# Reordering the border between a spiking recurrence and its score products: halves of the last copy of v, a short early count, and ScalarE's first output copies in a row

## The chip, the cores and the metric

The kernel runs on one core of a Trainium2 chip. The metric is the device time of one execution in microseconds, the median of several runs. One more execution is taken with a profiler, and everything that is read from a trace below comes from it.

## The reference

Sequences of 50 item numbers (1024 of them) are looked up in a table of 100001 rows of 128 values; row 0 counts as zero. The running means over time are normalised over the batch at each step, and drive a membrane that spikes. The mean spike count is multiplied with the whole table.

```python
emb = emb_table.at[0].set(0.0)
e = emb[seq]                                   # 1024 x 50 x 128
prefix = jnp.cumsum(e, axis=1)
denom = jnp.minimum(t_idx[None, :], lengths[:, None])
uF = prefix / denom[:, :, None]
y = (uF - uF.mean(axis=0)) * lax.rsqrt(uF.var(axis=0) + BN_EPS) * gamma + beta
def step(v, x):
    v = v + (x - v) / TAU                      # TAU = 2
    spike = (v - V_TH >= 0)                    # V_TH = 1
    v = v - spike * V_TH
    return v, spike
_, spikes = lax.scan(step, v0, y by time)
uF_out = spikes.mean(axis=0)                   # 1024 x 128
scores = uF_out @ emb.T                        # 1024 x 100001, float32
```

The scores are 409.6 MB, which is nearly all that the kernel writes.

## The kernel before

The work has two stages. In the first, a loop over t = 0 to 49 does the recurrence with the 128 features on the partitions and the 1024 sequences (B) in the columns. For each t, POOL gathers eight tiles of 128 rows (line 196), TensorE transposes and adds them into two PSUM banks pre0 and pre1 (line 310, 512 columns each), VectorE divides by the lengths into uF (line 319) and takes statistics (lines 320 and 326), ScalarE takes the square root r (line 330). VectorE then works out the scale a in a few instructions on one column, ScalarE writes x into a PSUM tile v (line 360), VectorE adds the old membrane (`step`, line 363). Three things are made of v: ScalarE's copy d = v − 1 as bf16 (`over`, line 282), VectorE's negv, which holds the reset membrane with its sign turned (`rest`, line 286), and VectorE's running count of spikes (`spiked`, line 289). In the loop, count and negv of step t are done during step t+1, behind other work. The v tiles alternate between the two PSUM tags v0 and v1, of two banks each; step 48 lies in v0.

The last step (t = 49) has its own order. The spikes of the first 128 sequences are worked out first (vA, countA), so that the first products can start; the next 512 (countB, through the bank of pre1) and the last 384 (countC, through a PSUM tile vC) follow. Before the products, TensorE does 16 transposes into a tile called warm, which nothing reads.

In the second stage, the table is taken in parts of 1024 rows: TensorE transposes them, ScalarE writes a high part (line 146) and VectorE a low part (line 147), and for each of eight groups n of 128 sequences, four matmuls of 512 columns (line 154, `product`) make a block of 128 × 1024 scores in PSUM. A block is copied out, times 1/50, by VectorE (line 486) or ScalarE (line 488) in turn, by the parity of the counter `turn`. The copies go into a tile o, and SP issues the store of it (line 163). Parts are taken in groups of WIDTHS = four of 2, four of 3 and thirteen of 6, and the loop over n is inside that over the groups, so a store carries 2, 3 or 6 blocks. Group n = 0 of the first two parts is done ahead, in halves of 512 columns, by `first_store` (lines 409 to 414): three of its copies on ScalarE, the fourth on VectorE. Its PSUM tiles are po_0_0 (tag po0) and po_0_1.

The order is written by hand (`manual_schedule`): each engine executes its instructions in the order of the program, and semaphores are added for what depends on another engine. The PSUM pool of the second stage has four buffers of two banks; they reuse the banks of the first stage, and each waits for the last user of what lay there.

## Time and profile before

| | |
|---|---|
| time, median of 3 runs | 1636.69 us (1634.44 to 1641.79) |
| profiled execution | 1575.79 us, of which the span is 1573.8 us |
| busy: PE, DVE, ACT, POOL | 1128.7, 944.8, 668.2, 380.4 us |
| output copies, line 486 (VectorE) and 488 (ScalarE) | 391 each, 1.22 and 1.02 us on average for one |
| HBM written, read | 409.60 MB, 77.69 MB |
| stores of 3 MB | 96, 20.0 us from issue to landing (median) |
| first store issued | 513.48 us after the span's start |

Engines: PE is TensorE's matmul, PEld its weight load, DVE is VectorE, ACT is ScalarE, POOL is GpSimd, SP issues the stores. A busy share over the whole span mixes the two stages; the stages have to be read apart. In the row of slices, each digit is the busy share in tenths of a fortieth of the span (39.3 us).

### The profile page before, as it was taken

To read this page: it belongs to the slowest core of one execution; us is meant where nothing else is said; L and a number is where in the kernel's file an instruction comes from. 1 tells how busy PE (TensorE), PEld (TensorE's weight loads), DVE (VectorE), ACT (ScalarE), POOL (GpSimd) and SP (SyncE) were. 2 spreads that over 40 slices of the span, in tenths; PEclk is the share of its full clock that TensorE was granted. 3 is DMA by queue.
4 is the path that set the end of the run, shared out by engine and by line. 5 is a ranking of instruction groups with operands and counts; after the bars stand their busy time and mean duration, and the time that the engine had idled before them with its cause. 6 is when DMAs were issued, how large, how long until landed. Compare 5 with 4: busy or idle time off the path is not lost.

```text
span 1573.8 us, 12233 instructions
## 1 busy us (share of the span) xinstructions
PE 1128.7 (72%) x4450; PEld 801.0 (51%) x4450; DVE 944.8 (60%) x1126; ACT 668.2 (42%) x697; POOL 380.4 (24%) x406
## 2 busy tenths in 40 slices
PE   4544444444444998889878878787888788888884
PEld 2211111111122776668666666666666666666663
DVE  5777777777777665567545545555555545555552
ACT  2333333333333554456444444444444444444542
POOL 7777777777776000000000000000000000000000
PEclk7555555555555999999999999999999999999998
DMA  9611111111121999999999999999999999999898
GB/s 349 235 52 54 52 54 52 53 53 53 52 80 45 373 415 404 422 416 403 422 427 432 431 427 425 421 413 432 412 429 425 413 428 410 426 413 425 379 426 371
DMA packets 51897, 488.12 MB, mean 310 GB/s; under 512 B 10075, under 2 KB 11004, under 8 KB 30588
## 3 DMA queue, kind: packets, MB, share of 16 engines
q1 hardware_dynamic: 30464, 429.81, 64.9%
q0 software_dynamic: 12800, 26.24, 5.7%
q10 hardware_dynamic: 8572, 31.28, 5.0%
q8 instruction: 35, 0.57, 0.1%
q14 instruction: 26, 0.21, 0.0%
HBM read 77.69 MB, written 409.60 MB: 310 GB/s over the span
## 4 chain that ended last, share of the span: by engine, by line
DMA 51%; POOL 18%; PE 11%; issue 8%; ACT 5%; DVE 3%; another core or an unknown queue 1%; ACTq 0%; SPq 0%; POOLq 0%; DVEq 0%
DMA scores<-o 46%; POOL e L196 18%; PE po L154 11%; DMA e<-in_L_rec_emb_table,idx 5%; ACT o L488 5%; DVE o L486 1%; PE pt L124 0%; ACT pairs L146 0%; DMA idx<-in_r_seq 0%; PE pre L310 0%; ACTq L116 0%; DVE negv L286 0%; DVE bs L320 0%; ACT hi L146 0%
## 5 line engine op out<-in xcount | busy, mean ns | idle before, releaser
L486 DVE TENSOR_SCALAR o<-po 128x1024 f32<-128x1024 f32 x391 | 464.2, 1221 | 346.5 <-DMA scores<-o 304.7
L488 ACT ACTIVATE o<-po 128x1024 f32<-128x1024 f32 (+1 forms) x391 | 389.4, 1018 | 542.5 <-DMA scores<-o 313.6
L196 POOL DMA_INDIRECT e<-in_L_rec_emb_table,idx x400 | 379.8, 949 | 123.8 <-issue 112.8
L154 PE MATMUL po<-pairs,countB 128*128 128x512 f32 x1136 | 305.4, 415 | 64.4 <-ACT o L488 49.2
L310 PE MATMUL pre<-ident,e 128*128 128x128 f32 x400 | 179.8, 462 | 228.9 <-DMA e<-in_L_rec_emb_table,idx 228.3
L154 PEld LDWEIGHTS po<-pairs,countB 128*128 128x128 f32 x1136 | 219.3, 198 | 127.8 <-ACT o L488 63.9
L154 PE MATMUL po<-pairs,countC 128*128 128x512 f32 x852 | 233.8, 421 | 46.6 <-ACT o L488 46.5
L310 PEld LDWEIGHTS pre<-ident,e 128*128 128x128 f32 x400 | 73.3, 184 | 338.8 <-DMA e<-in_L_rec_emb_table,idx 338.1
L154 PEld LDWEIGHTS po<-pairs,countC 128*128 128x128 f32 x852 | 165.2, 200 | 91.7 <-ACT o L488 57.6
L147 DVE TENSOR_TENSOR pairs<-pt,pairs 128x1024 fp32r<-128x1024 f32 x71 | 86.3, 1222 | 93.0 <-ACT pairs L146 93.0
L319 DVE SCALAR_TENSOR_TENSOR uF<-rlen,pre 128x512 f32<-128x512 f32 x100 | 68.3, 683 | 109.0 <-PE pre L310 108.9
L124 PE MATMUL pt<-ident,rows 128*128 128x128 f32 x782 | 110.5, 288 | 8.8 <-issue 4.9
L124 PEld LDWEIGHTS pt<-ident,rows 128*128 128x128 f32 x782 | 100.3, 151 | 27.1 <-issue 12.5
L330 ACT ACTIVATE r<-mv,eps 128x1 f32<-128x1 f32 x50 | 14.8, 295 | 225.0 <-DVE mv L326 225.0
L154 PE MATMUL po<-hi,countB 128*128 128x512 f32 x216 | 91.1, 422 | 18.1 <-ACT o L488 14.6
L270 PE MATMUL pre<-zT,ls 128*128 128x512 f32 x100 | 77.4, 776 | 23.5 <-DVE uF L319 19.6
L154 PE MATMUL po<-lo,countB 128*128 128x512 f32 x216 | 88.4, 411 | 0.0
L282 ACT ACTIVATE d<-v,less 128x1024 bf16<-128x1024 f32 x49 | 54.6, 1113 | 63.5 <-DVE v L363 63.5
L154 PE MATMUL po<-hi,countC 128*128 128x512 f32 (+1 forms) x162 | 68.1, 420 | 14.2 <-ACT o L488 14.1
L146 ACT CAST pairs<-pt 128x1024 fp32r<-128x1024 f32 x71 | 71.8, 1012 | 14.2 <-PE pt L124 14.2
L154 PE MATMUL po<-pairs,countA 128*128 128x512 f32 x284 | 71.3, 394 | 8.2 <-ACT o L488 8.2
L360 ACT ACTIVATE v<-uF,hgb,a 128x1024 f32<-128x1024 f32 x49 | 59.2, 1208 | 30.6 <-DVE a L356 30.5
(76 smaller groups left out, 819.3 us busy)
## 6 DMA issues: line engine op xcount, KB each, us to landing
scores<-o SPq DMA_DIRECT2D x96, 3072.0 KB, 20.0
scores<-o SPq DMA_DIRECT2D x32, 1536.0 KB, 8.9
scores<-o SPq DMA_DIRECT2D x30, 1024.0 KB, 8.0
rows<-in_L_rec_emb_table ACTq DMA_DIRECT2D x19, 1536.0 KB, 29.4
scores<-o SPq DMA_DIRECT2D x8, 2896.5 KB, 17.4
rows<-in_L_rec_emb_table SPq DMA_DIRECT2D x6, 3072.0 KB, 29.3
e<-in_L_rec_emb_table,idx POOLq DMA_INDIRECT x400, 2.5
rows<-in_L_rec_emb_table SPq DMA_DIRECT2D x1, 1024.0 KB, 5.1
```

The costliest lines, as they stand in the source:

```text
L124: nc.tensor.transpose(pt[:, k0 : k0 + kw], r[:kw, k0 : k0 + D], ident[:kw, :kw])
L146: nc.scalar.copy(vh, vp)
L147: nc.vector.tensor_tensor(vl, vp, vh.bitcast(F32), ALU.subtract)
L154: nc.tensor.matmul(po[:, :kw], lhsT=counts[n], rhs=part[:, k0 : k0 + kw], start=j == 0, stop=j == 1,)
L196: nc.gpsimd.indirect_dma_start(out=es[t][:, n * P : (n + 1) * P], out_offset=None, in_=table, in_offset=bass.IndirectOffsetOnAxis(ap=idx[: ...
L270: nc.tensor.matmul(pre[h], lhsT=l, rhs=zT[:, h * BANK : (h + 1) * BANK], start=t == 0, stop=False, skip_group_check=True,)
L282: nc.scalar.activation(d, v, AF.Identity, bias=less)
L310: nc.tensor.matmul(pre[h][:, k : k + P], lhsT=e[:, h * BANK + k : h * BANK + k + P], rhs=ident, start=False, stop=last, is_transpose=True, ...
L319: nc.vector.scalar_tensor_tensor(uF[:, cs], rlen[:, cs], 1.0 / (t + 1), pre[h], ALU.max, ALU.mult)
L360: nc.scalar.activation(vt, uF[:, cs], AF.Identity, bias=hgb[:, 1:2], scale=a)
L486: nc.vector.tensor_scalar_mul(o[:, h0 : h0 + hw], po[:, :hw], 1.0 / T)
L488: nc.scalar.mul(o[:, h0 : h0 + hw], po[:, :hw], 1.0 / T)
```

## The change

ScalarE's copy d of step 48 is made in two halves of 512 columns. In the last step, VectorE counts only the first 128 columns of step 48 at first, and makes negv in two halves, with near (which needs 128 columns of negv) between them. The counts of the other columns of step 48 come later: 512 columns after x of group B has been issued, 384 after the output copies of n = 0. Step 48's v stays in use until then, so the tile warm moves from the tag v0 to po0 (whose banks nothing else has used yet), po_0_1 from v0 to v1, and vC from v1 to v0. ScalarE issues x of group B, then its three output copies in a row, then x of vC; before, each x was followed by one copy. The counter `turn` starts at 1, so that of every pair of blocks ScalarE copies the first and VectorE the second.

```diff
@@ -276,20 +276,22 @@
                     skip_group_check=True,
                 )
 
+        whole = slice(0, B)
+        halves = [slice(h * BANK, (h + 1) * BANK) for h in range(B // BANK)]
+
         def over(t, v):
 
             d = lp.tile([P, B], BF16, tag="d", name=f"d_{t}")
-            nc.scalar.activation(d, v, AF.Identity, bias=less)
+            for cs in halves if t == T - 2 else (whole,):
+                nc.scalar.activation(d[:, cs], v[:, cs], AF.Identity, bias=less)
             return d
 
-        def rest(d, v):
-            nc.vector.scalar_tensor_tensor(negv, d, 0.0, v, ALU.is_ge, ALU.subtract)
+        def rest(d, v, cs):
+            nc.vector.scalar_tensor_tensor(negv[:, cs], d[:, cs], 0.0, v[:, cs], ALU.is_ge, ALU.subtract)
 
         def spiked(out, cs, v):
             nc.vector.scalar_tensor_tensor(out, v, V_TH, count[:, cs], ALU.is_ge, ALU.add)
 
-        whole = slice(0, B)
-        halves = [slice(h * BANK, (h + 1) * BANK) for h in range(B // BANK)]
         v = None
 
         correct(0, only(0))
@@ -299,10 +301,11 @@
             last = t == T - 1
             e = es.pop(t)
             if last:
-                spiked(count, whole, v)
-                rest(d, v)
+                spiked(count[:, :P], slice(0, P), v[:, :P])
+                rest(d, v, halves[0])
                 near = once.tile([P, P], F32, tag="r0", name="near")
                 nc.vector.tensor_scalar(near, negv[:, :P], -0.5, hgb[:, 1:2], ALU.mult, ALU.add)
+                rest(d, v, halves[1])
             uF = up.tile([P, B], F32, tag="uF", name=f"uF_{t}")
             bs = sp.tile([P, B // BANK, 6], F32, tag="bs", name=f"bs_{t}")
             for h, cs in enumerate(halves):
@@ -338,7 +341,7 @@
 
 
             if t and not last:
-                rest(d, v)
+                rest(d, v, whole)
 
             nc.vector.reciprocal(r, r)
             q = sp.tile([P, 1], F32, tag="q", name=f"q_{t}")
@@ -390,16 +393,15 @@
 
 
 
-        warm = vp.tile([P, HALF], F32, tag="v0", name="warm")
+        warm = accp.tile([P, HALF], F32, tag="po0", name="warm")
         for k in range(2 * KQ):
             nc.tensor.transpose(warm[:, k % KQ * P : (k % KQ + 1) * P], ident, ident)
-        vC = vp.tile([P, B - BANK - P], F32, tag="v1", name="vC")
-        groups = [(slice(P, P + BANK), pre[1], countB), (slice(P + BANK, B), vC, countC)]
-        for cs, vt, _ in groups:
+        po1 = vp.tile([P, HALF], F32, tag="v1", name="po_0_1")
+        pieceB, pieceC = slice(P, P + BANK), slice(P + BANK, B)
+        for cs in (pieceB, pieceC):
             nc.scalar.activation(uF[:, cs], uF[:, cs], AF.Identity, bias=mv[:, 0:1], scale=-1.0)
 
         po0 = accp.tile([P, HALF], F32, tag="po0", name="po_0_0")
-        po1 = vp.tile([P, HALF], F32, tag="v0", name="po_0_1")
         o0 = gp.tile([P, HALF], F32, tag="e", name="o_0_0")
         o1 = up.tile([P, HALF], F32, tag="uF", name="o_0_1")
         firsts = [(q, po, o, h, cs) for q, po, o in ((0, po0, o0), (1, po1, o1)) for h, cs in enumerate(halves)]
@@ -413,14 +415,17 @@
                 nc.scalar.mul(o[:, cs], po[:, cs], 1.0 / T)
             store(0, q * HALF + h * BANK, o[:, cs])
 
-        for k, (cs, vt, _) in enumerate(groups):
-            x(vt, cs)
-            first_store(*firsts[k])
-        for cs, vt, c in groups:
-            step(vt, cs)
-            spiked(c, cs, vt)
-        for f in firsts[2:]:
+        x(pre[1], pieceB)
+        spiked(count[:, pieceB], pieceB, v[:, pieceB])
+        step(pre[1], pieceB)
+        spiked(countB, pieceB, pre[1])
+        for f in firsts:
             first_store(*f)
+        spiked(count[:, pieceC], pieceC, v[:, pieceC])
+        vC = vp.tile([P, B - BANK - P], F32, tag="v0", name="vC")
+        x(vC, pieceC)
+        step(vC, pieceC)
+        spiked(countC, pieceC, vC)
 
 
 
@@ -429,7 +434,7 @@
         tc.tile_pool(name="psum", bufs=4, space=bass.MemoryType.PSUM, reuse_waits="tile")
     )
     opening = ExitStack()
-    turn = 0
+    turn = 1
     blocks = 0
     q0 = 0
     to_split = WIDTHS[0]
```

## The prediction

> **What bounds the kernel now.** I read the page first, then the busy time by stage, then the timeline of the few microseconds that the diff touches, then the chain of waits. From the page:

> ```profile
> span 1573.8 us, 12233 instructions
> POOL 7777777777776000000000000000000000000000
> DMA  9611111111121999999999999999999999999898
> ```

> A slice is 39.3 us. There are two stages: until slice 13 the gathers on POOL run and the DMA engines are nearly idle; then POOL stops and the DMA engines are full to the end, writing the 409.60 MB of scores. The change sits on the border. The busy time by stage shows how sharp the border is (the last two columns are DMA share and GB/s):

> ```profile
> 500.00:513.50 13.50, 8.13 (x30) 5.79 (x30) 10.80 (x22) 5.16 (x8) 3.77 (x4) 0.60 0.09 24
> 513.50:520.00 6.50, 5.57 (x24) 4.13 (x23) 4.69 (x7) 3.58 (x5) 0.00 (x0) 1.00 0.76 301
> 520.00:530.00 10.00, 10.00 (x54) 8.42 (x53) 7.06 (x7) 6.14 (x7) 0.00 (x0) 1.00 0.98 401
> 800.00:900.00 100.00, 83.40 (x359) 66.00 (x360) 54.45 (x46) 45.53 (x46) 0.00 (x0) 0.91 1.01 429
> ```

> From 520 us on the transfers set the end. So an edit at the border is worth exactly what it moves the time from which the DMA engines are continuously fed, and nothing more. In 513.5 to 522 us they lie idle for about 2.0 us (summed from narrower windows), so the feed starts, in effect, near 515.5 us. The timeline shows what leads up to it:

> ```profile
> 503.06 1.11 ACT L282 ACTIVATE d<-v,less 128x1024 bf16<-128x1024 f32 x1 [1.29 <-DVE v L363]
> 504.21 1.22 DVE L289 SCALAR_TENSOR_TENSOR count<-v,count 128x1024 bf16<-128x1024 f32 x1 [1.18 <-ACT d L282]
> 505.35 1.21 DVE L286 SCALAR_TENSOR_TENSOR negv<-d,v 128x1024 f32<-128x1024 bf16 x1
> 506.37 0.48 PE L310 MATMUL pre<-ident,e 128*128 128x128 f32 x1 [0.77 <-DMA e<-in_L_rec_emb_table,idx]
> 506.59 0.29 DVE L305 TENSOR_SCALAR near<-negv,hgb 128x128 f32<-128x128 f32 x1
> 506.61 3.28 PEld L395 LDWEIGHTS warm<-ident 128*128 128x128 f32 x16
> 506.80 0.68 DVE L319 SCALAR_TENSOR_TENSOR uF<-rlen,pre 128x512 f32<-128x512 f32 x1
> 508.12 0.67 DVE L319 SCALAR_TENSOR_TENSOR uF<-rlen,pre 128x512 f32<-128x512 f32 x1
> 509.56 0.21 DVE L326 BATCH_NORM_AGGREGATE mv<-bs 128x2 f32<-128x12 f32 x1
> 511.22 0.29 DVE L289 SCALAR_TENSOR_TENSOR countA<-vA,count 128x128 fp32r<-128x128 f32 x1
> 512.86 0.60 ACT L413 ACTIVATE o<-po 128x512 f32<-128x512 f32 x1 [0.38 <-PE po L154]
> 513.35 0.67 ACT L360 ACTIVATE vC<-uF,hgb,a 128x384 f32<-128x384 f32 x1
> 515.12 0.68 DVE L411 TENSOR_SCALAR o<-po 128x512 f32<-128x512 f32 x1
> 515.86 0.50 PE L154 MATMUL po<-hi,countB 128*128 128x512 f32 x1 [0.68 <-DVE o L411]
> ```

> Columns are start, duration, engine and line; the bracket is the idle time before and its releaser. DVE is the bound from 504.21 to 511.5: the eighth transpose of step 49 ends at 506.85, so DVE could read the first half of pre earlier (its transposes ended near 501.9) but is busy with count and negv. Note the 1.18 us in which count waits for ScalarE's d, although it does not use d: both read v.

> [...] the granted clock is 0.60 in 500 to 513.5 us and 1.00 after, so the warm transposes (506.64 to 510.29) must stay where they are, and they do.

> **The change, part by part.**

> 1. *Halved d, short count, halved negv.* Half a d: ScalarE's 1024-column eviction takes 1.03 and its 512-column one 0.60, so 512 columns are 0.43; d's first half ends at 503.06 + 1.11 − 0.43 = 503.74, the second near 504.25 (ScalarE instructions of 512 follow each other in 0.49). So the extra instruction costs 0.1 us at most. On DVE, a 128-column operation holds the engine 0.2 us (near to uF: 506.59 to 506.80), a 512-column one about 0.61 (bs to uF: 507.51 to 508.12). Old queue: count, negv, near from 504.21 to 506.80. New queue: count of 128 (0.23), negv half 0 (0.68, its end is awaited), near (0.21), negv half 1 (0.61), so uF comes 1.76 after the start. The unknown is the start. If count's 128 columns wait for d's first half alone: 503.77, uF at 505.52, second uF at 506.84, but its transpose ends at 506.85, so 506.89: a gain of 508.12 − 506.89 = **1.23**. If they wait for all of d: 504.28, uF 506.04, second uF 507.35: a gain of **0.77**. A hint for the latter: the first output copy (512.86) reads what two products wrote, yet starts when the fourth ends (512.82). A wait there covers a whole tile. I take 0.77 and keep 1.23 as the other bound.
> 2. *warm in po0's banks* removes its wait for negv; it still follows the last transpose. It caps the gain: countA's first matmul (511.66 before) cannot start before warm's end, 510.29, so at most 1.37. Not binding.
> 3. *Rest of count later.* 512 columns (0.61) go into DVE's 0.93 us wait for x of group B: free. The other 384 (0.56) come after VectorE's own output copy, and only vC waits for them.
> 4. *ScalarE's copies in a row.* x(vC) (0.67) leaves its place between the first and second copy. The copies would begin at 512.09, 512.58 and 513.07 (each 0.49; the third needs the eighth product, 513.74 − 0.77 = 512.97), against 512.86, 513.95 and 514.42. VectorE's fourth copy no longer stands behind vC and countC: 513.70 against 515.12. Stores on SP's queue keep their number and order and come 0.77 to 1.4 earlier.
> 5. *The price: vC is late.* It lies in v's old banks, so it waits for the 384-column count: count 514.3, x 514.9 to 515.5, step 515.55, countC 516.15 to 516.70 against 515.21 before. Behind x(vC) on ScalarE stands the copy of block n=1, q=0; behind countC on DVE stands q=1's. PE needs countC first at 523.13, so the count itself has 6 us to spare.
> 6. *turn = 1* swaps the 391 + 391 output copies: q=0 goes to ScalarE (515.55 to 516.57; VectorE ended it at 516.94 before), q=1 to VectorE after countC (516.70 to 517.95, against 518.17). Then n=2: ScalarE 516.7 to 517.7, VectorE 517.9 to 519.1. Its 1 MB store goes at about 519.15 instead of 519.95, and from there the DMA engines are fed. Each group's last copy becomes 1.22 instead of 1.03; a 3 MB store takes about 20 us to land (7.3 at 429 GB/s alone), so two others are queued and hide 0.2. The very last store has no cover: about +0.1.

> Sum: −0.8 + 0.1, about **−0.8** (−1.3 with the other bound). The profiled execution took 1575.79 with a span of 1573.8, and would take 1575.0. The median of the runs shown is 60.9 above it; that lies outside the profile, and I carry the difference over: 1636.69 − 0.8 = **1635.9**.

> **Rivals.**

> *A PSUM buffer takes the place of the wait that went.* Four output buffers lie over the eight banks. Before, the second product of n=1 took the buffer whose last reader was VectorE's fourth copy (last line above, 0.68 us). Were it the same banks again, they now hold vC, and PE waits for countC at 516.2 to 516.7; q=1's copy ends at 518.8, n=2's store goes at 520.65 to 521.1 instead of 519.95: +0.7 to +1.2, **1637.6**, slower. It decides once countC ends later than about 515.5. For it: the same banks were second in line. Against: which buffer is taken is not in the trace.

> *The swap breaks the steady state.* If the 0.2 us of the last copy were not hidden, the 160 stores from the second group on would cost 0.2 each: +32, **1669**. It decides when less than 4.5 us of transfers (the time from a freed buffer to its store, on the chain) is queued. Against: shares of 0.95 to 1.01 in every stretch of 50 us or more from 520 to 1550, and two queued stores. The other way, the stalls that an altered order could close are small: 2.0 us in 710 to 720, 1.1 in 596 to 606 (0.57 share in 1460 to 1470 has stores queued and is the transfers' own).

> *The transfers swallow it*: earlier first stores only widen the gap before n=1, **1636.7**.

> **How the numbers follow.** Forecast 0.5, buffer 0.3, swallowed 0.12, swap slower 0.05, an unknown gain from the swap 0.03. The three runs shown spread over 7.4 us, 0.45%, so 0.5% (8 us) is about what a measurement can tell from no change; all but the last two cases lie inside it. Scatter alone may carry a median out: faster 0.05, same 0.89, slower 0.06. The range takes −1.3 to +1.2 and about 4 to 5 us for the scatter: 1630.5 to 1641.5.

> **What would show it.** Right: d in two rows of 0.7; count's 128 columns at 503.8 or 504.3; second uF at 506.9 to 507.4; first store issued at 512.2 to 512.8 (513.48 before); DMA share near 1 from about 519; later stages alike. Wrong: PE idle over 1 us before n=1's second product with countC as releaser (the buffer rival), or shares under 0.95 after 530 (the swap).

## The result and the profile after

The changed kernel is slower. Over 19 runs each, the median is 1642.73 us against 1638.18; the ratio is 1.0032, with a 95% interval of 1.0020 to 1.0045, so 5.2 us (3.3 to 7.4); the two medians alone differ by 4.55 us. The forecast was 1635.9 with a range to 1641.5. A second comparison gave 1578.63 against 1576.15, ratio 1.0018 (1.0011 to 1.0026), 2.8 us (1.7 to 4.1).

Absolute times can be read only inside one comparison: in some of them the first stage of every kernel, the one before included, is some 60 to 70 us longer, with pauses of POOL between gathers (POOL is idle for 181.8 us before its gathers in the first profile after, for 123.8 in that of before). The profile of before shown above is of the short kind and the first profile after of the long kind; none of before is of the long kind. I therefore count from the end of step 48's v (503.03 us in that profile of before, 564.26 in the one after) and call this "after v".

The timeline of the changed kernel around the border, in order of time, columns as before:

```profile
564.30 1.26 ACT L286 ACTIVATE d<-v,less 128x512 bf16<-128x512 f32 x2 [1.30 <-DVE v L366]
565.05 3.30 PE L398 MATMUL warm<-ident 128*128 128x128 f32 x16
565.60 0.29 DVE L293 SCALAR_TENSOR_TENSOR count<-v,count 128x128 bf16<-128x128 f32 x1 [1.33 <-ACT d L286]
568.64 0.67 DVE L322 SCALAR_TENSOR_TENSOR uF<-rlen,pre 128x512 f32<-128x512 f32 x1
572.17 0.77 PE L154 MATMUL po<-hi,countA 128*128 128x512 f32 x1 [3.82 <-DVE a L355]
572.73 0.63 PE L154 MATMUL po<-lo,countA 128*128 128x512 f32 x1
576.59 0.69 DVE L413 TENSOR_SCALAR o<-po 128x512 f32<-128x512 f32 x1 [2.14 <-ACT o L415]
577.84 0.67 ACT L363 ACTIVATE vC<-uF,hgb,a 128x384 f32<-128x384 f32 x1 [1.28 <-DVE count L293]
579.14 0.56 DVE L293 SCALAR_TENSOR_TENSOR countC<-vC,count 128x384 fp32r<-128x384 f32 x1
579.75 0.50 PE L154 MATMUL po<-hi,countB 128*128 128x512 f32 x1 [2.12 <-DVE countC L293]
579.81 1.03 ACT L493 ACTIVATE o<-po 128x1024 f32<-128x1024 f32 x1 [1.30 <-DVE countC L293]
```

What is to be seen: the short count starts 0.04 us after both halves of d are done, and the second uF starts at 4.38 after v against 5.09 before. So the first part of the change brings 0.71 us. Then two things eat it. TensorE idles 3.82 us before its first product and works at half clock when it comes (0.50 in the table below; 0.63 us for a matmul where before had 0.39). And countC ends at 15.44 after v instead of 12.18; TensorE waits 2.12 us for it before n=1's second product (the four matmuls of its block q=1), and ScalarE waits 1.30 us for it before its first copy of n=1. The stage table of the same kernel says it in two columns (granted clock and DMA share, the third and second from the end):

```profile
572.00:574.00 2.00, 1.83 (x4) 1.49 (x5) 1.63 (x5) 0.78 (x1) 0.00 (x0) 0.50 0.00 0
574.00:576.00 2.00, 2.00 (x6) 1.60 (x5) 0.45 (x1) 1.13 (x3) 0.00 (x0) 0.50 0.13 50
578.00:580.00 2.00, 0.25 (x1) 0.25 (x2) 1.12 (x2) 0.70 (x2) 0.00 (x0) 0.97 0.40 154
580.00:582.00 2.00, 2.00 (x10) 1.60 (x10) 1.02 (x1) 0.93 (x2) 0.00 (x0) 1.00 0.16 63
```

The mark that counts is the store of n=2, the seventh that SP issues: from there on the transfers set the time. In the changed kernel it is this line, 19.85 after v; before it was at 16.93.

```profile
584.11 0.33 SPq L163 DMA_DIRECT2D scores<-o  x1
```

From the seventh store to the end of the span, before took 1573.8 − 519.96 = 1053.8 us and the changed kernel 1637.8 − 584.11 = 1053.7. In all 16 profiles of this study that stretch is 1053.5 to 1054.5. So nothing of the loss lies in the second stage, and 2.9 us of it lie in this profile between v and the seventh store.

### The profile page after: what moved, and what is told of

It reads as the page before. It is cut to its first block, busy times and chain, and to the rows that moved or that the text cites. A ratio compares the mean times of both kernels' runs of the same rounds, so it can differ in the third digit from the quotient of the medians.

```text
span 1637.8 us, 12235 instructions
## 1 busy us (share of the span) xinstructions
PE 1089.5 (67%) x4450; PEld 815.5 (50%) x4450; DVE 947.8 (58%) x1129; ACT 673.1 (41%) x698; POOL 380.8 (23%) x406
## 3 DMA queue, kind: packets, MB, share of 16 engines
HBM read 77.69 MB, written 409.60 MB: 298 GB/s over the span
## 4 chain that ended last, share of the span: by engine, by line
DMA 43%; DVE 18%; PE 15%; another core or an unknown queue 9%; ACT 5%; issue 5%; POOL 4%; ACTq 0%; SPq 0%; DVEq 0%; POOLq 0%
DMA scores<-o 39%; PE po L154 14%; POOL e L196 4%; DVE uF L322 3%; DVE bs L323 3%; DVE o L491 3%; DVE v L366 3%; ACT o L493 2%; DVE negv L290 2%; DMA rows<-in_L_rec_emb_table 2%; DVE count L293 1%; DMA e<-in_L_rec_emb_table,idx 1%; ACT v L363 1%; DVE pairs L147 1%
## 5 line engine op out<-in xcount | busy, mean ns | idle before, releaser
L491 DVE TENSOR_SCALAR o<-po 128x1024 f32<-128x1024 f32 (+1 forms) x391 | 467.5, 1214 | 326.5 <-DMA scores<-o 178.6
L493 ACT ACTIVATE o<-po 128x1024 f32<-128x1024 f32 x391 | 391.7, 1025 | 498.4 <-DMA scores<-o 354.6
L196 POOL DMA_INDIRECT e<-in_L_rec_emb_table,idx x400 | 380.1, 950 | 181.8 <-issue 107.0
L154 PE MATMUL po<-pairs,countB 128*128 128x512 f32 x1136 | 302.3, 412 | 56.1 <-ACT o L493 56.1
L154 PE MATMUL po<-pairs,countC 128*128 128x512 f32 x852 | 241.3, 428 | 60.4 <-ACT o L493 52.8
L154 PEld LDWEIGHTS po<-pairs,countB 128*128 128x128 f32 x1136 | 217.7, 196 | 117.1 <-ACT o L493 72.7
L154 PEld LDWEIGHTS po<-pairs,countC 128*128 128x128 f32 x852 | 167.6, 204 | 111.3 <-ACT o L493 64.5
L270 PEld LDWEIGHTS pre<-zT,ls 128*128 128x128 f32 x100 | 29.2, 293 | 322.3 <-DVE uF L322 290.6
L313 PE MATMUL pre<-ident,e 128*128 128x128 f32 x400 | 122.6, 434 | 69.8 <-DMA e<-in_L_rec_emb_table,idx 47.9
L313 PEld LDWEIGHTS pre<-ident,e 128*128 128x128 f32 x400 | 80.7, 210 | 113.1 <-DMA e<-in_L_rec_emb_table,idx 73.2
L154 PE MATMUL po<-hi,countB 128*128 128x512 f32 x216 | 90.3, 418 | 17.7 <-ACT o L493 15.5
L154 PE MATMUL po<-lo,countB 128*128 128x512 f32 x216 | 87.3, 406 | 0.0
L286 ACT ACTIVATE d<-v,less 128x1024 bf16<-128x1024 f32 (+1 forms) x50 | 54.7, 1096 | 63.5 <-DVE v L366 38.9
L154 PE MATMUL po<-hi,countC 128*128 128x512 f32 (+1 forms) x162 | 68.8, 425 | 14.6 <-ACT o L493 12.6
L363 ACT ACTIVATE v<-uF,hgb,a 128x1024 f32<-128x1024 f32 x49 | 59.2, 1208 | 30.9 <-DVE a L359 14.8
```

What stands on the lines that cost most here:

```text
L154: nc.tensor.matmul(po[:, :kw], lhsT=counts[n], rhs=part[:, k0 : k0 + kw], start=j == 0, stop=j == 1,)
L196: nc.gpsimd.indirect_dma_start(out=es[t][:, n * P : (n + 1) * P], out_offset=None, in_=table, in_offset=bass.IndirectOffsetOnAxis(ap=idx[: ...
L270: nc.tensor.matmul(pre[h], lhsT=l, rhs=zT[:, h * BANK : (h + 1) * BANK], start=t == 0, stop=False, skip_group_check=True,)
L286: nc.scalar.activation(d[:, cs], v[:, cs], AF.Identity, bias=less)
L313: nc.tensor.matmul(pre[h][:, k : k + P], lhsT=e[:, h * BANK + k : h * BANK + k + P], rhs=ident, start=False, stop=last, is_transpose=True, ...
L363: nc.scalar.activation(vt, uF[:, cs], AF.Identity, bias=hgb[:, 1:2], scale=a)
```

## The experiments

My theory: the loss is the late seventh store, from half clock at the first products and from the wait for countC. The rivals: countC alone, and the swap of the output copies (turn = 1). The table collects what was measured; "store" is the seventh store after v in the one profile of each kernel, with its difference to before's 16.93 (a second profile of before has 16.91); "time" is the measured ratio to before in the same comparison, over 13 to 22 runs of the kernel and 19 to 75 of before, and the same in us with its 95% interval.

| kernel | clock at the first products | countC ends | store | time against before |
|---|---|---|---|---|
| changed | 0.50 | 15.44 | 19.85, +2.9 | 1.0032, +5.2 (3.3 to 7.4) |
| changed, second comparison (a_again) | 1.00 | 13.83 | 18.22, +1.3 | 1.0018, +2.8 (1.7 to 4.1) |
| b_warm | 0.50 | 13.05 | 17.89, +1.0 | 0.9999, −0.2 (−2.1 to 1.8) |
| a_near | 1.00, then 0.50 | 14.36 | 18.74, +1.8 | 1.0017, +2.8 (1.0 to 4.8) |
| a_turn0 | 0.50 | 15.43 | 20.92, +4.0 | 1.0027, +4.4 (2.6 to 6.2) |
| a_near_sbuf | 1.00 | 12.93 | 16.25, −0.7 | 1.0006, +1.0 (−0.8 to 2.8) |
| a_near_sbuf_2 | 1.00 | 12.93 | 16.27, −0.7 | 1.0000, 0 (−1.3 to 1.4) |
| b_again | 1.00 | 12.17 | 16.91, 0 | 0.9999, −0.2 (−1.4 to 1.3) |
| b_turn1 | 0.50 | 13.05 | 18.13, +1.2 | 1.0001, +0.2 (−1.3 to 1.4) |
| a_sbuf | 0.50 | 14.54 | 17.87, +0.9 | 1.0003, +0.5 (−0.8 to 1.7) |
| best | 1.00 | 11.71 | 15.79, −1.1 | 0.9993, −1.1 (−2.4 to 0.2) |
| a_near22 | 1.00 | 14.20 | 20.19, +3.3 | 1.0018, +2.8 (1.7 to 3.9) |
| best22 | 1.00 (steps up in the first) | 12.41 | 16.51, −0.4 | 0.9994, −0.9 (−2.4 to 0.3) |
| a_order | 0.50 | 12.34 | 16.79, −0.1 | 1.0000, 0 (−2.5 to 2.5) |
| b_halves | 1.00, then 0.50 | 11.48 | 16.55, −0.4 | 0.9997, −0.5 (−2.3 to 1.3) |

**b_warm**: before, with warm early.

```diff
-        warm = vp.tile([P, HALF], F32, tag="v0", name="warm")
+        warm = accp.tile([P, HALF], F32, tag="po0", name="warm")
```

> The kernel before with one line changed: the tile warm takes the tag po0 instead of v0, so its 16 transposes no longer wait for negv. Clock theory (the change is slower because warm runs too early, the array idles over 3 us before countA's first product, and the products then run at half clock): warm ends about 4 us and more before the first product, the products of n=0 stand 0.43 us apart instead of 0.23, the third output copy comes some 1.6 us later, 1 to 2.5 us slower than before. Buffer theory (only countC's wait costs) and swap theory (only turn=1 costs): the same as before within 0.5 us.

In its profile, warm ends at 0.3 after v, 8.3 us before the first product, and all of n=0 runs at half clock (0.50); the store comes 1.0 us late. The time does not show the 1 to 2.5 us that the clock theory expected (−2.1 to 1.8). Half clock behind an early warm is there; what it costs alone is under 2 us and not shown in the time.

**a_near**: the changed kernel, with warm held until near is written.

```diff
-            nc.tensor.transpose(warm[:, k % KQ * P : (k % KQ + 1) * P], ident, ident)
+            nc.tensor.transpose(warm[:, k % KQ * P : (k % KQ + 1) * P], near, ident)
```

> The changed kernel, but the 16 warm transposes take near as their input instead of the identity, so that they start only when VectorE has written near. What they write is read by nobody. Clock theory: warm starts about 2 us later than in the changed kernel, the clock stays at 1.0 through the first products (0.23 us apart), the third output copy comes 1.6 us earlier, and the kernel is 1.5 to 2 us faster than the changed one, so about 3 us slower than before if the whole loss is 5. Buffer and swap theories: as slow as the changed kernel, ratio 1.003.

Warm starts at 2.60 instead of 0.79 after v and the first four of the eight matmuls of n=0 run at full clock (1.00), the last ones at half (0.50); the store moves from 19.85 to 18.74. The ratio falls from 1.0032 to 1.0017, but the intervals overlap, so the time does not establish the expected gain of 1.5 to 2 us. Slower than before it remains: half clock at the first products is not the whole cause.

**a_turn0**: the changed kernel with `turn = 0`.

> The changed kernel with turn = 0, so that the output copies fall to the engines as they did before. Swap theory (the loss beyond the 2.9 us seen at the border comes from the order of 782 copies): 2 us or more faster than the changed kernel. Clock and buffer theories: the same as the changed kernel within 1 us, ratio 1.003; the second stage, from the store of n=2 to the end, lasted 1053.8 us before and 1053.7 after, which speaks against the swap.

Still 4.4 us slower. The swap theory falls here; b_turn1 below settles it. Its store is the latest of all; in this profile the clock costs twice: n=0 runs at half clock (0.50), the wait for countC is 2.93 us here, and the matmuls behind it are at half clock again (0.63 us).

**a_near_sbuf**, and **a_near_sbuf_2** in another comparison: a_near's edit and

```diff
-        vC = vp.tile([P, B - BANK - P], F32, tag="v0", name="vC")
+        vC = once.tile([P, B - BANK - P], F32, tag="vC", name="vC")
```

> The changed kernel with two edits: warm takes near as its input (as in the other run), and vC is a tile in SBUF instead of PSUM banks 6 and 7, so that the buffer of n=1's second product waits for the 384-column count only and not for countC. Clock and buffer theories together: both losses at the border go (1.6 and about 1.2 to 2 us), and the earlier first output copies are left: n=2's store about 16.2 us after step 48's v, against 16.95 before and 19.8 in the changed kernel; 0.5 to 1 us faster than before. Swap theory: still about 2 us slower than before.

> The changed kernel with warm fed by near and vC in SBUF, a second time, since the first comparison (1.0006, -0.0005 to 1.0017) could not tell 0.7 us faster from 1 us slower. Border theory: 0.3 to 0.8 us faster than before and 2 to 3 us faster than the changed kernel. If ScalarE's copies in a row cost more than the border shows: slower than before.

The wait of the second product shrinks to 0.50 us (it starts at 11.93 after v, when the 384-column count has ended), x of vC no longer waits for that count, and the store goes 0.7 us earlier than before. ScalarE's first copy of n=1 still waits for countC, 1.77 us, so that wait is not one for vC's PSUM banks. In the quieter of the two comparisons the kernel is level with before (−1.3 to 1.4). Against the changed kernel in the same comparison the 2.8 us are gone. Since a_near alone still loses 2.8 us, it is the move of vC into SBUF that takes the loss away. The 0.7 us of gain are neither shown nor excluded.

**b_again**: before, unchanged.

> The kernel before once more, as a measure of what two equal kernels differ by, and for a profile whose first stage is as long as in the other runs (the first profile of before had a first stage some 57 us shorter). All theories: ratio 1.000 within 0.001. Clock theory: warm starts right after negv, 3.6 us after step 48's v, and ends about 1.5 us before the first product, so the products of n=0 stand 0.23 us apart at least at first; n=2's store goes about 17 us after v.

Two equal kernels differ by 0.2 us. Its first stage is short like that of the first profile, so I did not get the long kind that I wanted; its border is the same to 0.02 us.

**b_turn1**: before with `turn = 1`.

> The kernel before with turn = 1 and nothing else: the swap of the output copies alone. The four kernels with the changed border measured 1 to 2.3 us more than the shift of n=2's store in their profiles explains. Swap theory: 1.5 to 2.5 us slower than before, the second stage (from n=2's store to the end) longer by as much. Border theory (clock and countC alone): the same as before within 1 us; n=2's store at about the same time after v.

The swap costs nothing (−1.3 to 1.4). The profile brought something else: up to the first products this kernel has the same instructions as b_again, warm begins 3.7 us after v in both and ends over 1 us ahead of the products in both (1.26 and 1.76), and yet b_again ran them at full (1.00) and b_turn1 at half clock (0.50). The stage tables, first b_turn1 and then b_again, clock in the third column from the end:

```profile
511.00:513.00 2.00, 1.36 (x3) 1.16 (x4) 1.04 (x4) 0.98 (x2) 0.00 (x0) 0.50 0.00 0
513.00:515.00 2.00, 2.00 (x6) 1.55 (x5) 0.96 (x3) 1.28 (x3) 0.00 (x0) 0.50 0.00 0
```

```profile
511.00:513.00 2.00, 0.71 (x3) 0.65 (x4) 1.11 (x5) 1.52 (x3) 0.00 (x0) 1.00 0.00 0
513.00:515.00 2.00, 1.73 (x8) 1.11 (x8) 1.71 (x3) 1.63 (x4) 0.00 (x0) 1.00 0.02 7
```

So the clock at the border differs from one execution to the next. In the traces of before and after, each of the 140 whole stretches of one granted clock is a multiple of 3.41 us long, from 1 to 124 of them. Where the steps lie differs: before steps up at 7.72 after v, after at 3.63, 4.09 us apart, which is no multiple. Two stretches of 3.41 us in b_turn1 and then two in b_again (after the length comes TensorE's busy time, the clock is again third from the end):

```profile
505.38:508.79 3.41, 2.62 (x12) 2.33 (x13) 3.33 (x6) 0.00 (x0) 0.00 (x0) 0.50 0.08 19
508.79:512.20 3.41, 2.15 (x9) 1.69 (x8) 2.53 (x10) 1.93 (x4) 0.00 (x0) 0.50 0.00 0
```

```profile
506.51:509.92 3.41, 2.83 (x13) 2.83 (x14) 3.31 (x6) 0.00 (x0) 0.00 (x0) 0.50 0.00 1
509.92:513.34 3.42, 1.66 (x10) 1.29 (x10) 2.27 (x11) 2.19 (x4) 0.00 (x0) 1.00 0.00 0
```

Warm lasts 3.6 and 3.2 us here, about one such stretch. In b_again TensorE is busy for 2.83 us of the first, and the clock goes from 0.50 to 1.00 at its end. In b_turn1 warm (506.76 to 510.38) lies across both, TensorE is busy for 2.62 and 2.15 us of them, and the clock is 0.50 in both. A single profile of the border therefore carries 1 to 1.6 us of luck (b_warm and b_turn1 come 1.0 and 1.2 us behind b_again, the first profile after 1.6 us behind a_again), which fits b_turn1, whose store is late and whose time is not.

**a_sbuf**: the changed kernel with vC in SBUF alone.

> The changed kernel with vC in SBUF, warm still early: takes the wait of n=1's second product for countC away, and leaves the half clock. With a_near and a_near_sbuf it makes a square. Clock and buffer theories: n=2's store about 1.2 to 1.7 us later than in a_near_sbuf (the products of n=0 at 0.43 us), so some 17.6 us after v; 1.0 to 2 us slower than a_near_sbuf, ratio to before about 1.0015. If the clock didn't matter: as a_near_sbuf, 1.0006.

Half clock (0.50), and TensorE's wait is 0.76 us, for the 384-column count and no longer for countC: +0.9 by the store, +0.5 in time. With a_near (full clock, 1.00, at first, the wait stays, +2.8) it completes the square. By the store the wait is the larger term: 2.0 us (19.85 to 17.87), against 1.6 for the clock (19.85 to 18.22 in a_again below, the same kernel at full clock). In time the two intervals, −0.8 to 1.7 and 1.0 to 4.8, overlap a little.

**best**: a_near_sbuf's edits, and after x of B the order

```diff
+        vC = once.tile([P, B - BANK - P], F32, tag="vC", name="vC")
         x(pre[1], pieceB)
         spiked(count[:, pieceB], pieceB, v[:, pieceB])
+        first_store(*firsts[0])
+        x(vC, pieceC)
         step(pre[1], pieceB)
         spiked(countB, pieceB, pre[1])
-        for f in firsts:
-            first_store(*f)
+        first_store(*firsts[1])
         spiked(count[:, pieceC], pieceC, v[:, pieceC])
-        vC = vp.tile([P, B - BANK - P], F32, tag="v0", name="vC")
-        x(vC, pieceC)
         step(vC, pieceC)
         spiked(countC, pieceC, vC)
+        for f in firsts[2:]:
+            first_store(*f)
```

> A version meant to keep the gain and lose the losses: the changed kernel with warm fed by near and vC in SBUF, and with ScalarE's x of C and copies in the order of before (x, copy, x, copy), the 384-column count directly behind countB, so that countC ends near 12.0 us after v (12.18 before, 15.44 in the changed kernel). Border theory: n=2's store about 16.2 us after v or less, 0.7 us faster than before and 0.3 to 1 us faster than a_near_sbuf, ratio 0.9996. Swap theory (turn is 1 here too): 1 to 1.5 us slower than before.

Its timeline, VectorE and TensorE:

```profile
513.69 0.55 DVE L293 SCALAR_TENSOR_TENSOR count<-v,count 128x384 bf16<-128x384 f32 x1
514.74 0.56 DVE L293 SCALAR_TENSOR_TENSOR countC<-vC,count 128x384 fp32r<-128x384 f32 x1
514.86 0.39 PE L154 MATMUL po<-hi,countB 128*128 128x512 f32 x1
```

The second product of n=1 (514.86) follows the first without a wait, and the store goes at 15.79. The time is 1.1 us less than before, as the store says, but the interval (0.9985 to 1.0001) just reaches 1, so "faster" is likely and not established.

**a_again**: the changed kernel, in the comparison with a_near_sbuf_2.

> The changed kernel once more, next to the versions below on one chip. Border theory with countC: n=2's store at 18.2 us after v where the array is at full clock at the first products and up to 19.8 where it is not; 1.2 to 2.9 us slower than before. A theory that puts the 5 us of the first comparison down to the change itself wherever it runs: 4 to 6 us slower.

Here the first products ran at full clock (1.00), so the wait stands alone:

```profile
514.35 0.69 DVE L413 TENSOR_SCALAR o<-po 128x512 f32<-128x512 f32 x1 [0.54 <-ACT o L415]
515.60 0.67 ACT L363 ACTIVATE vC<-uF,hgb,a 128x384 f32<-128x384 f32 x1 [1.28 <-DVE count L293]
517.51 0.50 PE L154 MATMUL po<-hi,countB 128*128 128x512 f32 x1 [2.45 <-DVE countC L293]
517.57 1.03 ACT L493 ACTIVATE o<-po 128x1024 f32<-128x1024 f32 x1 [1.30 <-DVE countC L293]
```

The idle time is 2.45 us; the store is 1.3 late with the clock at 1.00 and 2.9 in the other profile, at 0.50, and the time, 2.8 (1.7 to 4.1), is within what a mixture of the two gives.

**a_near22** and **best22**: a_near and best with `range(22)` in place of `range(2 * KQ)` for warm.

> The changed kernel with warm fed by near and with 22 transposes instead of 16, so that the array is busy until just before the first product. The profiles so far show that the granted clock steps from 0.50 to 1.00 some 3 to 7 us after warm's start, or not before the products at all. Clock theory: the clock is 1.00 at the first product in nearly every execution, n=2's store 18.2 us after v; about 1 us faster than the changed kernel, still 1 us slower than before, since countC's wait stays. If the clock at the border doesn't matter: as the changed kernel.

> The version meant to be the best (before's order of x and copies, early 384-column count, vC in SBUF, warm fed by near) with 22 warm transposes. Clock theory: 0.3 to 0.8 us faster than the version with 16, so 1.5 us or more faster than before. If the 6 more transposes only delay the first product: up to 0.7 us slower than the version with 16.

What the clock theory expected missed in both: a_near22 is as slow as the changed kernel, and best22 is no faster than best, as the other branch had it (its store is 0.7 us later). With the longer warm the products of n=0 do run at full clock (1.00; in best22 from the middle of the first), and it holds the first of them back: 8.28 and 8.71 after v instead of 7.91. In a_near22 the clock then falls again: behind the gap that countC makes, a matmul takes 0.63 us where it took 0.40 ahead of it:

```profile
514.25 0.40 PE L154 MATMUL po<-lo,countB 128*128 128x512 f32 x1
517.46 0.67 PE L154 MATMUL po<-hi,countB 128*128 128x512 f32 x1 [2.81 <-DVE countC L293]
517.92 0.63 PE L154 MATMUL po<-lo,countB 128*128 128x512 f32 x1
518.35 0.63 PE L154 MATMUL po<-hi,countB 128*128 128x512 f32 x1
```

So the wait can cost twice: as idle time (2.81 us here), and as half clock behind it (0.50).

**a_order**: the changed kernel, the order after x of B put back, vC still in PSUM.

```diff
         x(pre[1], pieceB)
         spiked(count[:, pieceB], pieceB, v[:, pieceB])
+        spiked(count[:, pieceC], pieceC, v[:, pieceC])
+        vC = vp.tile([P, B - BANK - P], F32, tag="v0", name="vC")
+        first_store(*firsts[0])
+        x(vC, pieceC)
+        first_store(*firsts[1])
         step(pre[1], pieceB)
         spiked(countB, pieceB, pre[1])
-        for f in firsts:
-            first_store(*f)
-        spiked(count[:, pieceC], pieceC, v[:, pieceC])
-        vC = vp.tile([P, B - BANK - P], F32, tag="v0", name="vC")
-        x(vC, pieceC)
         step(vC, pieceC)
         spiked(countC, pieceC, vC)
+        for f in firsts[2:]:
+            first_store(*f)
```

> The changed kernel, with only the order after x of group B put back: the 384-column count goes ahead of vC at once, and ScalarE does x, copy, x, copy, copy as before. vC stays in PSUM in v's old banks, warm and turn stay as changed. Order theory (countC is late because it stands behind three copies): countC ends near 12 us after v instead of 13.8 to 15.4, PE's wait before n=1's second product shrinks to under 1 us, and the kernel is level with before or up to 0.7 us faster (ratio 0.9995 to 1.0005). Bank theory (vC in the banks of n=1's second product costs whatever the order): 1.5 us or more slower than before.

countC ends at 12.34 and the store goes at 16.79, at half clock (0.50) even. The interval of the time is wide (−2.5 to 2.5), so it is the profile that answers: with vC in the same banks, TensorE no longer waits before n=1's second product. The order theory holds: countC was late because it stood behind the copies.

**b_halves**: before with the first part of the change alone, warm fed by near, and the count's other 896 columns right after warm's place (the halves of d and the columns in `rest` are as in the change and left out here).

```diff
-                spiked(count, whole, v)
-                rest(d, v)
+                spiked(count[:, :P], slice(0, P), v[:, :P])
+                rest(d, v, halves[0])
                 near = once.tile([P, P], F32, tag="r0", name="near")
                 nc.vector.tensor_scalar(near, negv[:, :P], -0.5, hgb[:, 1:2], ALU.mult, ALU.add)
+                rest(d, v, halves[1])
...
-        warm = vp.tile([P, HALF], F32, tag="v0", name="warm")
+        warm = accp.tile([P, HALF], F32, tag="po0", name="warm")
...
-            nc.tensor.transpose(warm[:, k % KQ * P : (k % KQ + 1) * P], ident, ident)
+            nc.tensor.transpose(warm[:, k % KQ * P : (k % KQ + 1) * P], near, ident)
...
+        spiked(count[:, P:], slice(P, B), v[:, P:])
```

> The kernel before with the first part of the change alone: d of step 48 in halves, 128 columns counted early, negv in halves, the other 896 columns counted after a, while VectorE waits for x; warm in po0 and fed by near, since v is still in use. Order of copies, vC's and po_0_1's banks and turn as before. If the 0.71 us of that part arrive at the end: first store 9.7 us after v instead of 10.45, 0.3 to 0.7 us faster than before (ratio 0.9996 to 0.9998; 896 columns hold VectorE 0.95 us, about what its wait for x offers). If the transfers swallow it: 1.0000.

First store at 9.75 after v as expected (10.45 before), seventh at 16.55. The time (−2.3 to 1.3) cannot tell 0.4 us.

## Why the prediction was wrong

*What held.* The end is set by when the DMA engines are fed: the stretch from the seventh store on is the same to 1 us in all 16 profiles (1053.5 to 1054.5). Step 1 held with the bound that I took: the short count waited for all of d, and the second uF came 0.71 us earlier where I had 0.77. Step 6, the swap: no cost in the steady state shows (b_turn1, −1.3 to 1.4). In the clean profile, a_again, the first copies begin at 9.11, 9.60 and 10.08 after v (my step 4 had 9.06, 9.55 and 10.04).

*The step that failed is 5 with 6*: "Behind x(vC) on ScalarE stands the copy of block n=1, q=0" was the whole price I set, and countC "has 6 us to spare". It had none. countC has two more waiters: TensorE, since n=1's second product takes the banks in which vC lies, and ScalarE's first output copy of n=1, which waits 1.30 us for countC in both profiles of the changed kernel. That copy writes an SBUF tile of the second stage; since it waits for countC with vC out of PSUM too, the wait is, by my estimate, one for SBUF bytes that the first stage used, but which bytes the traces do not say. I had let the copy of q=0 start at 12.5 after v, ahead of countC's end; it started at 13.94. The buffer rival named the first of these waiters, with its sign and nearly its size (+0.7 to +1.2; a_again shows +1.3). I gave it 0.3, although the bracket of 0.68 us in the profile of before showed those banks as second in line; that was the evidence to follow.

*Step 2 failed as well*: "it still follows the last transpose" took that transpose's place from one profile, where it ended 3.8 after v. In other executions it ends at 1.0 after v or before v, and warm, freed from negv, runs with it. It then ends 3.8 us or more ahead of the products, and they run at half clock (0.50 in after, a_turn0, a_order and b_warm). The granted clock of 1.00 that I read at the products, to which before stepped up 0.46 us after warm's end, is one draw, as b_turn1 showed; that b_turn1 has half clock (0.50) with a late warm, 3.7 us after v, shows that the place of warm alone does not decide. Half clock adds about 1.6 us to the store (18.22 to 19.85).

*Smaller readings.* The 60.9 us that I carried over do not lie outside the profile: they are the longer first stage, which that one profile of before did not have (in the first profile after, v ends 61.2 us later). The four terms of the new queue in step 1 add up to 1.73 us, not 1.76 (measured: 1.72). And one stretch of 50 us in before, 1420 to 1470, has a DMA share of 0.93, not 0.95 or more.

*What stays open.* The first comparison's 3.3 to 7.4 us lies above the 2.9 of its profile, the second's 1.7 to 4.1 agrees with 1.3 to 2.9. That TensorE is at half clock more often where the first stage is long would fit, but it is not shown: I have at most two profiles of a kernel and cannot count it; and before has no profile with the long first stage, so the 2.9 us compare a long with a short one.

## What to carry to other kernels

When an instruction is moved later, list everything that waits for it through memory, the next user of its PSUM banks and of its SBUF bytes included, and not only those who read its result: here a count with 6 us to spare for its reader had none for its banks. A filler that is to have TensorE at full clock has to be tied to the time at which the work comes, not to the time at which the array becomes free: with warm fed by near, the clock is 1.00 at the first product, or reaches it within that product, in all seven profiles; with warm in po0 and fed by the identity, in one of six. A filler of 3.6 us is still no guarantee, as b_turn1 shows (0.50, warm behind negv). And where one stage is bound by its transfers, take the store behind which the rest always takes the same time as the mark, and measure each variant by it. It shows which wait a variant has moved where the times cannot, but compare only profiles with the same clock at the border: half clock alone shifts it by 1 to 1.6 us, and the rest varies by up to 1 us.

## What I had not expected of the hardware

```profile
564.48:567.89 3.41, 3.11 (x15) 3.11 (x16) 2.26 (x5) 1.08 (x2) 0.00 (x0) 0.50 0.00 0
567.89:571.31 3.42, 0.46 (x4) 0.23 (x2) 3.21 (x10) 0.99 (x3) 0.00 (x0) 1.00 0.00 0
571.31:574.72 3.41, 2.55 (x6) 2.10 (x7) 2.70 (x7) 1.67 (x3) 0.00 (x0) 0.50 0.00 0
574.72:578.13 3.41, 2.91 (x7) 1.70 (x6) 1.16 (x2) 1.50 (x4) 0.00 (x0) 0.50 0.60 229
```

The clock steps up at 567.89, with warm almost done (3.11 us of work), falls at 571.31 after 3.41 us with 0.46 us of work, 0.86 us ahead of the first product, and steps up once more at 578.13, while TensorE waits for countC.

Two gaps came out differently as well. A gap of 2.81 us brought 0.63 us matmuls after it in a_near22, while after 2.45 us in a_again they stayed at 0.39. In a_near22 the clock fell at 517.63, after 3.41 us with 0.60 us of work:

```profile
514.22:517.63 3.41, 0.60 (x3) 0.17 (x2) 2.27 (x4) 0.83 (x3) 0.00 (x0) 1.00 0.80 303
517.63:521.05 3.42, 3.42 (x9) 2.65 (x10) 1.23 (x1) 0.91 (x1) 0.00 (x0) 0.50 0.38 153
```

In a_again the granted clock is 1.00 from 516 to 520, with 0.49 us of work in the first two of these four. Whether the length of a gap decides, or where it lies to the steps, is not shown.
